# The rounding number of an FP4 quantiser: two VectorE passes, or one ScalarE pass and a fused maximum

## The chip, the core and the metric

The kernel runs on one core of a Trainium2 chip. A core has five engines that run side by side, each through its own queue of instructions: TensorE (PE in the profile; its weight loads are PEld), VectorE (DVE), ScalarE (ACT), GpSimd (POOL) and SyncE (SP, which here only issues DMAs). The metric is the device time of one execution in microseconds, the median of several runs.

## The reference, cut to what matters

The input x has 16 batches of 512 rows of 256 values. Each row is normalised to xn. From xn come two results: s, a layer of attention with 16 heads followed by a feed-forward layer with GELU, and g, a gated feed-forward layer in which every operand is first rounded to FP4 in blocks of 16 values. The output is x + s * g.

```python
xn = _layernorm(x, axis=-1)
s = _L0_attn_ref(xn, ...)                      # attention, then ffn_w1, gelu, ffn_w2
g = _silu(_L0_ffn_ref(xn, w_gate, w_up, w_down))
x = x + s * g

def fp4_quant_dequant(x):                      # blocks of 16
    scale = jnp.maximum(jnp.max(jnp.abs(xb), axis=-1, keepdims=True) / 6.0, 1e-12)
    xn = xb / scale
    idx = jnp.searchsorted(_MID, jnp.abs(xn))  # _MID 0.25, 0.75, 1.25, 1.75, 2.5, 3.5, 5
    q = _GRID[idx] * jnp.sign(xn) * scale      # _GRID 0, 0.5, 1, 1.5, 2, 3, 4, 6

gate, y = fp4_linear(x, w_gate), fp4_linear(x, w_up)
return fp4_linear(jax.nn.silu(gate) * y, w_down)   # 704 hidden columns
```

The part at issue is the rounding to the grid. After division by its block's scale a value lies between -6 and 6, and the grid's step there is 0.5 below 2, 1 from 2 to 4 and 2 above 4.

## The kernel before, in words

The work is cut into 64 steps. Step s handles batch b = s // 4 and g = s % 4; g counts both four heads of the attention and one of the four tiles of 128 rows of the gated layer. In the same step the previous batch ("old") goes through the later parts of its layer: its attention output and first normalisation at g = 0 and 1, the expansion by ffn_w1 with GELU (`expand`) at g = 1 and 2, and the contraction by ffn_w2 at g = 2 and 3.

One step goes like this. TensorE first multiplies the attention weights of the step before with the values (`context`, tile cp), and ScalarE copies that out (`kept`, tile ct). Then come five bursts: the scores of this step (`weights`: tile ws, of which there is one buffer; ScalarE takes its exponential into pr, and GpSimd multiplies pr by a table, `tabled`), and the scores of the next step (`maxima`: tile ms; VectorE takes its maxima, whose throw-away output is called junk). Between bursts the letters of a plan (`PLAN[g]`) put other pieces, such as the transposes ctp and ct of `output`, xqtp of `turned_x` and hqtp of `turned_hidden`. At the end of the step come the gated layer's two halves (`hidden`: tiles gp, up and gu; ScalarE's Silu writes sl, VectorE multiplies into wide), the first stage of their quantiser, the product with the down weights of the step before (`gate`: tile dp, ScalarE writes gated), for g = 1 and 2 of an old batch `expand`, then a dummy exponential (`expect`, tile ready) that has the table for Exp loaded in good time, and last the remaining stages of the quantiser.

The quantiser is `fp4_stages`, a generator in four stages. It takes the block maxima (amax) and their reciprocal (inv) on VectorE and multiplies by inv on GpSimd (L222); then it makes the rounding number m, adds it, subtracts it, and multiplies by the block's scale on GpSimd (L232). Adding and subtracting a large number rounds a value to that number's last place, so m has to follow the value's size: m is the value's power of two, but at least 1, times 6291456. VectorE makes it in two passes, a bitwise "and" that keeps the exponent (L226) and a maximum with a multiplication (L227). In `ROUNDING`, three of the four tiles of a batch have the addition and the subtraction on VectorE ("dd"); the fourth (g = 3) has the subtraction on GpSimd ("dg"). The tile m has one buffer for all quantisers.

The quantiser works on the hidden values (tile wide, 128 x 704) once in every step; on the inputs of the gated layer (tile xq, 128 x 512, two row tiles at once) in every second step, started at g = 1 and g = 2; and on the weights (tiles wide and raw_d) while the kernel starts up.

What sets the order: TensorE issues in the order in which the program is written throughout, and from step 0 on VectorE and ScalarE do too (`dve.fixed = act.fixed = True`). An instruction that waits on one of these engines therefore holds up all that follow it there. GpSimd, SyncE, and the start-up before step 0 are ordered by a scheduler at build time. Nearly all instructions of the three ordered engines pass through one helper, so the profile shows them with its line, L72, and they are told apart by their tiles.

Of the kernel before, what the change touches and what calls it, by code (L numbers as in the profile page):

```python
# [11 lines left out]

F32 = mybir.dt.float32
I32 = mybir.dt.int32
F32R = mybir.dt.float32r
BF16 = mybir.dt.bfloat16
AF = mybir.ActivationFunctionType
ALU = mybir.AluOpType
# [7 lines left out]
I_FF = 704  # L26
D_FF = 4 * D
ALPHA, MIX, STEP_A = 3.0, 0.15, 6.0
P = 128
# [12 lines left out]

ROUND = 12582912.0
TURN = 6.283185
LEVEL = 6291456.0
EXPONENT = 0x7F800000
UNDER = 1.0 + 2.0**-22


# [1 line left out]
def tile_block(ctx: ExitStack, tc: tile.TileContext, a: dict, pos: bass.AP, win: bass.AP, out: bass.AP):  # L51
    nc = tc.nc
# [21 lines left out]
    pe, dve, act = InOrder(nc.tensor, True), InOrder(nc.vector, False), InOrder(nc.scalar, False)  # L74
# [20 lines left out]
    sb = ctx.enter_context(tc.tile_pool(name="sb", bufs=1))  # L95
# [82 lines left out]
    NF = D_FF // P  # L178
# [14 lines left out]

    v_aug = [keep.tile([P, NT, H, VS], F32, name=f"va{i}", tag=f"va{i}") for i in range(2)]

    def fp4_stages(dst, src, n, width, engines=(dve, dve)):

        nb = width // 16
        widest = 2 * D if width <= 2 * D else I_FF

        def temporary(name, columns):
            return sb.tile([P, widest // columns], F32, name=f"{name}{widest}", tag=f"{name}{widest}")[
                :n, : width // columns
            ]

        amax, scale, inv = (temporary(x, 16) for x in ("amax", "scale", "inv"))

        def blocks(t):
            return t.rearrange("p (n k) -> p n k", k=16)

        def per_block(t):
            return t.unsqueeze(2).to_broadcast([n, nb, 16])

        dve.tensor_reduce(amax, blocks(src), AX.X, ALU.max, apply_absolute_value=True)
        dve.tensor_scalar(inv, amax, UNDER / 6.0, UNDER * 1e-12, ALU.mult, ALU.max)  # L220
        dve.reciprocal(inv, inv)
        nc.gpsimd.tensor_tensor(blocks(dst), blocks(src), per_block(inv), ALU.mult)  # L222
        nc.gpsimd.tensor_scalar(scale, amax, 1.0 / 6.0, 1e-12, ALU.mult, ALU.max)  # L223
        yield
        m = sb.tile([P, I_FF], F32, name="m", tag="m")[:n, :width]
        dve.tensor_scalar(m.bitcast(I32), dst.bitcast(I32), EXPONENT, None, ALU.bitwise_and)  # L226
        dve.tensor_scalar(m, m, 1.0, LEVEL, ALU.max, ALU.mult)  # L227
        yield
        engines[0].tensor_tensor(dst, dst, m, ALU.add)
        yield  # L230
        engines[1].tensor_tensor(dst, dst, m, ALU.subtract)
        nc.gpsimd.tensor_tensor(blocks(dst), blocks(dst), per_block(scale), ALU.mult)  # L232

    def fp4(dst, src, n, width):
        for _ in fp4_stages(dst, src, n, width):
            pass
# [9 lines left out]
    def bank(name):  # L246
        return ps.tile([P, 512], F32, name=name, tag="mm")
# [335 lines left out]
    def turned_h(b, h, half):  # L583
        hT = sb.tile([P, NC, 2 * P], F32, name=f"hT_{b}_{half}", tag="hT")
        tp = bank(f"htp_{b}_{half}")
        for c in range(NC):
            for t in range(2):
                turn(tp[:, (2 * c + t) * P : (2 * c + t + 1) * P], rows_of(h, 2 * half + t)[:, c * P : (c + 1) * P])
        act.copy(hT.rearrange("p c t -> p (c t)"), tp)
        return hT  # L590

    def expand(b, half, hT):

        acts = []
        for f in range(NF):
            fp = bank(f"f1_{b}_{half}_{f}")
            for c in range(NC):
                mm(fp[:, : 2 * P], w1[:, c, f * P : (f + 1) * P], hT[:, c, :], start=(c == 0), stop=(c == NC - 1))
            acts.append(sb.tile([P, 2 * P], F32, name=f"act_{b}_{half}_{f}", tag="act", bufs=NF + 2))
            act.activation(acts[f], fp[:, : 2 * P], AF.Gelu, bias=fb1[:, f : f + 1])  # L600
        return acts
# [33 lines left out]

    HI = I_FF // 2

    ROUNDING = [[dve if e == "d" else nc.gpsimd for e in by] for by in ("dd", "dd", "dd", "dg")]

    def quantised(b, t):  # L640

        xq = sb.tile([P, 2, D], F32, name=f"xq_{b}_{t}", tag="xq", bufs=2)
        src = xns[b][t // 2].rearrange("p t d -> p (t d)")
        return xq, fp4_stages(xq.rearrange("p t d -> p (t d)"), src, P, 2 * D)
# [10 lines left out]
    def hidden(b, t, xqT):  # L655

        hid = wide[t % 2]

        def halves():
            for s in range(2):  # L660
                cut = slice(s * HI, (s + 1) * HI)
                if s == 1:
                    both = ps_s.tile([P, 2, S], F32, name=f"gu_{b}_{t}", tag="ws")
                    gp, up = both[:, 0, :], both[:, 1, :]
                else:
                    gp, up = bank(f"gp_{b}_{t}"), bank(f"up_{b}_{t}")
                for wT, acc in ((wgT, gp), (wuT, up)):
                    for c in range(NC):
                        mm(
                            acc[:, :HI],  # L670
                            xqT[:, c * P : (c + 1) * P],
                            wT[:, c, cut],
                            start=(c == 0),
                            stop=(c == NC - 1),
                        )
                sl = sb.tile([P, HI], F32, name=f"sl_{b}_{t}_{s}", tag="sl", bufs=2)
                act.activation(sl, gp[:, :HI], AF.Silu)
                dve.tensor_tensor(hid[:, cut], up[:, :HI], sl, ALU.mult)
                yield

        return hid, halves(), fp4_stages(hid[:, :I_FF], hid[:, :I_FF], P, I_FF, ROUNDING[t])

    def turned_hidden(b, t, hq):
        hqT = sb.tile([P, NI, P], F32, name=f"hqT_{b}_{t}", tag="hqT")
# [15 lines left out]
    def expect(function):  # L700

        act.activation(ready, mhalf[:, 0:1], function)
# [291 lines left out]
    for k in range(H // 2 + 2):  # L994
# [14 lines left out]
        if 0 < k < H // 2 + 1:  # L1009
            tag, bufs = (("pr1", 1), ("gated", 2))[k % 2]  # L1010
# [26 lines left out]
    xq, stages = quantised(0, 0)  # L1037
# [66 lines left out]
    waiting, hq, cts, turned_hs, acts, coming, mv = None, None, [], {}, {}, None, None  # L1104
    xqTs, hqTs = {}, {}
    xqs = {0: xq}
    stages = iter(())
# [4 lines left out]
    for s in range(STEPS):  # L1112
        b, g = divmod(s, H // 4)
        old, has_old = b - 1, b > 0
# [61 lines left out]
        if pair and pair[0] < B:  # L1176
            xqs[(4 * pair[0] + pair[1]) // 2], more = quantised(*pair)
            next(more)
        hq, halves, stages = hidden(b, g, xqTs.pop((b, g)))
        before = (b, g)  # L1180
        ops = ahead
# [19 lines left out]
        if gating:  # L1201
            gate(*gating, hqTs.pop(gating))
        if has_old and g in (1, 2):
            acts[g - 1] = expand(old, g - 1, turned_hs[g - 1])
        if not has_old:
            for _ in stages:
                pass
# [3 lines left out]
        if s == NT - 1:  # L1211
            for w, name in ((w1, "ffn_w1"), (w2, "ffn_w2")):
                nc.sync.dma_start(out=w, in_=a[name].rearrange("(c p) n -> p c n", p=P))
        expect(AF.Exp)
        if s + 2 < STEPS:
            ahead = operands(*divmod(s + 2, H // 4))
# [4 lines left out]
    old = B - 1  # L1221
# [14 lines left out]
    hT = turned_h(old, h, 0)  # L1236
# [5 lines left out]
    for half in range(2):  # L1242
        acts[half] = expand(old, half, hT)
        if half == 0:
            hT = turned_h(old, h, 1)
        for i, _ in enumerate(contract(old, h, half, acts[half], mv, 1)):
            if i % 4 < 3:
                continue
            caught_up()
            t = 2 * half + i // 4  # L1250
            rs = sb.tile([P, 2], F32, name=f"rs_last_{t}", tag="rs2")
            inverse_deviation(rs[:, :1], mv[:, t : t + 1, 1])
            layernorm(rows_of(h, t), mv[:, t, 0:1], rs[:, :1], g2, b2)
            gt = gated[:, t, :]
            dve.tensor_tensor(gt, gt, rows_of(h, t), ALU.mult)
            dve.tensor_tensor(gt, gt, x_last[:, t, :], ALU.add)
            nc.sync.dma_start(out=out[old, t * P : (t + 1) * P, :], in_=gt)
# [43 lines left out]
```

## Time and profile before

| | |
|---|---|
| runs | 1875.64, 1875.63 and 1872.88 us, median 1875.63 us |
| span of the profiled execution, first to last instruction | 1872.6 us |
| TensorE busy, share of the span | 1774.8 us, 95% |
| VectorE busy | 1423.1 us, 76% |
| GpSimd busy | 1310.3 us, 70% |
| ScalarE busy | 1069.1 us, 57% |
| ScalarE table loads | 168, 215.5 us |
| rounding number on VectorE, 704 columns ("and"; maximum and product) | 65 x 854 ns; 66 x 809 ns |
| addition or subtraction, 704 columns, VectorE | 114 x 907 ns |
| subtraction on GpSimd (L231) | 16 x 1686 ns |

The page of the profile gives the profiled execution's span and not its total time; the span lies 0.28 us below the fastest of the three runs and 3.03 us below their median, so what lies around the span is at most about 3 us. A mean over the whole span mixes the start-up (until about 300 us), the repeating stretch of about 106 us for each batch, and the ending (the last 63 us). The lines of waits say which engine sat idle and which engine's instruction ended it; the idle time of an engine costs something only if the end of the kernel waits for it.

### The profile page before, as it was taken

Reading aid. Unit: us, or ns where it says so; the run is one execution under the profiler, and the core shown is the slowest. Engines: PE = TensorE matmul, PEld = TensorE weight load, DVE = VectorE, ACT = ScalarE, POOL = GpSimd, SP = SyncE. Lnnn points to the kernel's source line nnn. Section 1 sums busy time; section 2 is a strip of 40 time slices with the busy share of each in tenths; the row PEclk is TensorE's granted clock in tenths of the full one; section 3 lists DMA queues with packets and bytes.
Section 4 is the critical chain, followed back from the end, with each engine's and each line's share of the span. In section 5 each row is a group of like instructions: output and inputs, shape, how many; then the busy total and the mean of one; then the engine's idle time right before and its main releaser. Section 6 shows DMA issues by size and latency. Waiting matters only on the chain.

```text
span 1872.6 us, 31762 instructions
## 1 busy us (share of the span) xinstructions
PE 1774.8 (95%) x10411; PEld 1240.5 (66%) x10411; DVE 1423.1 (76%) x3887; ACT 1069.1 (57%) x1853; POOL 1310.3 (70%) x1128
## 2 busy tenths in 40 slices
PE   5679799999999999999999999999999999999998
PEld 2235467676776767676776767677676767677676
DVE  5878587787878777787878777787878778787754
ACT  5654455655665555556565565556555565565553
POOL 5467477767776776777676776777677776777671
PEclk8869799999999999999999999999999999999999
DMA  6344242432323242422334242332333242232200
GB/s 203 95 148 134 81 129 68 138 87 88 109 89 120 68 126 80 137 84 76 112 95 127 60 135 81 117 101 76 112 94 109 73 138 86 77 108 79 72 21 12
DMA packets 127114, 184.68 MB, mean 99 GB/s; under 512 B 15315, under 2 KB 57749, under 8 KB 126949
## 3 DMA queue, kind: packets, MB, share of 16 engines
q1 hardware_dynamic: 122496, 181.25, 32.2%
q8 instruction: 83, 1.36, 0.3%
q10 hardware_dynamic: 4004, 0.98, 0.3%
q14 instruction: 83, 0.67, 0.1%
q0 software_dynamic: 448, 0.42, 0.1%
HBM read 136.45 MB, written 45.09 MB: 97 GB/s over the span
## 4 chain that ended last, share of the span: by engine, by line
PE 81%; DVE 8%; POOL 1%; issue 1%; ACT 1%; DMA 0%; DVEq 0%; POOLq 0%; ACTq 0%
PE f L72 25%; PE dp L72 8%; PE gu L72 8%; PE cp L72 7%; PE ws L72 5%; DVE junk L72 4%; PE op L72 4%; PE gp L72 4%; PE up L72 4%; PE ms L72 4%; PE vp L72 3%; PE hqtp L72 2%; DVE cx L72 1%; PE qk_wk L72 1%; PE qk_wq L72 1%
## 5 line engine op out<-in xcount | busy, mean ns | idle before, releaser
L500 POOL TENSOR_TENSOR pr<-pr,table 128x1024 f32<-128x1024 f32 (+2 forms) x448 | 768.0, 1748 | 75.2 <-ACT pr L72 73.0
L72 DVE CUSTOM_DVE_ANT_0 junk<-ms,mask 128x512 bf16<-128x512 f32 (+3 forms) x1024 | 501.9, 490 | 231.9 <-PE ms L72 155.0
L72 ACT ACTIVATE pr<-ws 128x1024 f32<-128x1024 f32 (+1 forms) x350 | 327.0, 955 | 134.4 <-PE ws L72 129.1
L72 ACT ACT_TABLE_LOAD x168 | 215.5, 1283 | 64.3 <-PE gp L72 48.8
L72 PE MATMUL f<-w,act 128*128 128x256 f32 x1024 | 249.0, 387 | 0.0
L72 PE MATMUL f<-hT,w 128*128 128x256 f32 x1024 | 226.3, 380 | 0.0
L72 PEld LDWEIGHTS f<-hT,w 128*128 128x128 f32 x1024 | 194.8, 190 | 26.3 <-ACT hT L72 0.2
L72 PEld LDWEIGHTS f<-w,act 128*128 128x128 f32 x1024 | 187.0, 190 | 31.3
L232 POOL TENSOR_TENSOR wide<-wide,scale 128x704 f32<-128x704 f32 (+1 forms) x71 | 96.6, 1361 | 136.5 <-DVE wide L72 132.9
L72 PE MATMUL ws<-qT,kT 38*128 38x512 f32 (+3 forms) x1024 | 157.5, 371 | 21.4 <-ACT pr L72 16.5
L72 PE MATMUL dp<-wdT,hqT 128*128 128x256 f32 x768 | 176.2, 379 | 0.0
L72 PEld LDWEIGHTS dp<-wdT,hqT 128*128 128x128 f32 x768 | 146.1, 190 | 31.1 <-issue 6.7
L72 ACT ACTIVATE act<-f,fb 128x256 f32<-128x256 f32 x256 | 118.2, 474 | 75.3 <-PE f L72 72.5
L72 PE MATMUL ms<-kT,qT 36*128 36x512 f32 (+3 forms) x1024 | 145.1, 330 | 9.5 <-DMA kT<-k_d 6.3
L72 PE MATMUL cp<-pr,va 128*17 128x512 f32 (+3 forms) x2048 | 151.5, 434 | 0.0
L72 PEld LDWEIGHTS ws<-qT,kT 38*128 38x128 f32 x1024 | 81.6, 188 | 90.8 <-issue 51.7
L72 PEld LDWEIGHTS cp<-pr,va 128*17 128x17 f32 x2048 | 54.3, 97 | 99.4 <-issue 79.5
L223 POOL TENSOR_SCALAR scale<-amax 128x32 f32<-128x32 f32 (+1 forms) x104 | 37.0, 356 | 116.6 <-DVE amax L72 113.5
L72 DVE TENSOR_TENSOR wide<-wide,m 128x704 f32<-128x704 f32 (+2 forms) x126 | 112.4, 892 | 4.1
L222 POOL TENSOR_TENSOR wide<-wide,inv 128x704 f32<-128x704 f32 (+1 forms) x71 | 99.1, 1396 | 21.5 <-DVE inv L72 21.1
L72 PEld LDWEIGHTS ms<-kT,qT 36*128 36x128 f32 x1024 | 96.2, 189 | 18.4 <-issue 12.8
L72 DVE TENSOR_SCALAR m<-m 128x512 f32<-128x512 f32 (+1 forms) x104 | 102.6, 986 | 3.4
(217 smaller groups left out, 3009.5 us busy)
## 6 DMA issues: line engine op xcount, KB each, us to landing
table<-rv SPq DMA_DIRECT2D x64, 1024.0 KB
kT<-k_d SPq DMA_DIRECT2D x256, 76.0 KB
qT<-q_d SPq DMA_DIRECT2D x256, 72.0 KB
x<-in_L_attn_x_dram SPq DMA_DIRECT2D x21, 512.0 KB
q_d<-q_hi SPq DMA_DIRECT2D x32, 256.0 KB
q_d<-q_lo SPq DMA_DIRECT2D x32, 256.0 KB
k_d<-k_hi SPq DMA_DIRECT2D x32, 256.0 KB
k_d<-k_lo SPq DMA_DIRECT2D x32, 256.0 KB
```

The source lines that it names most:

```text
L72: return lambda *args, **kw: self.follow(op(*args, **kw))
L222: nc.gpsimd.tensor_tensor(blocks(dst), blocks(src), per_block(inv), ALU.mult)
L223: nc.gpsimd.tensor_scalar(scale, amax, 1.0 / 6.0, 1e-12, ALU.mult, ALU.max)
L232: nc.gpsimd.tensor_tensor(blocks(dst), blocks(dst), per_block(scale), ALU.mult)
L500: nc.gpsimd.tensor_tensor(part, part, table[:, mine, j * P :], ALU.mult)
```

## The change

ScalarE makes the rounding number: one activation, the absolute value with the scale 4194304, written in bfloat16. The floor that the maximum gave moves into VectorE's addition and subtraction, which become fused instructions of the form (m max 5242880) op value. The subtraction now yields the negative of the rounded value, so GpSimd makes the block's scale negative. `ROUNDING` is gone; both fused instructions are on VectorE in every step. ScalarE's instruction is also given a place of its own in the step: with g = 1 and 2 of an old batch it stands between the fourth and the fifth GELU of `expand`; with g = 0 and 3 it stands after `gate` and ahead of the dummy exponential; in the first batch it runs with the rest of the quantiser, behind `gate`. The quantiser of xq runs its stages where it did, so there the new instruction stands on ScalarE behind the second Silu of `hidden`.

```diff
-LEVEL = 6291456.0
-EXPONENT = 0x7F800000
+LEVEL = 4194304.0
...
-        nc.gpsimd.tensor_scalar(scale, amax, 1.0 / 6.0, 1e-12, ALU.mult, ALU.max)
+        nc.gpsimd.tensor_scalar(scale, amax, -1.0 / 6.0, -1e-12, ALU.mult, ALU.min)
         yield
-        m = sb.tile([P, I_FF], F32, name="m", tag="m")[:n, :width]
-        dve.tensor_scalar(m.bitcast(I32), dst.bitcast(I32), EXPONENT, None, ALU.bitwise_and)
-        dve.tensor_scalar(m, m, 1.0, LEVEL, ALU.max, ALU.mult)
+        m = sb.tile([P, I_FF], BF16, name="m", tag="m")[:n, :width]
+        act.activation(m, dst, AF.Abs, scale=LEVEL)
         yield
-        engines[0].tensor_tensor(dst, dst, m, ALU.add)
+        dve.scalar_tensor_tensor(dst, m, 1.25 * LEVEL, dst, ALU.max, ALU.add)
         yield
-        engines[1].tensor_tensor(dst, dst, m, ALU.subtract)
+        dve.scalar_tensor_tensor(dst, m, 1.25 * LEVEL, dst, ALU.max, ALU.subtract)
         nc.gpsimd.tensor_tensor(blocks(dst), blocks(dst), per_block(scale), ALU.mult)
...
-    def expand(b, half, hT):
+    def expand(b, half, hT, between=iter(())):
         acts = []
         for f in range(NF):
+            if f == NF // 2:
+                next(between, None)
...
-    ROUNDING = [[dve if e == "d" else nc.gpsimd for e in by] for by in ("dd", "dd", "dd", "dg")]
...
-        return hid, halves(), fp4_stages(hid[:, :I_FF], hid[:, :I_FF], P, I_FF, ROUNDING[t])
+        return hid, halves(), fp4_stages(hid[:, :I_FF], hid[:, :I_FF], P, I_FF)
...
-            acts[g - 1] = expand(old, g - 1, turned_hs[g - 1])
+            acts[g - 1] = expand(old, g - 1, turned_hs[g - 1], stages)
...
+        if not has_old or g % 3 == 0:
+            next(stages, None)
         expect(AF.Exp)
```

More of the change, by code (lines that the diff above doesn't have):

```diff
@@ L13 @@
 F32 = mybir.dt.float32
-I32 = mybir.dt.int32
 F32R = mybir.dt.float32r
@@ L194, in tile_block, with fp4_stages @@
     v_aug = [keep.tile([P, NT, H, VS], F32, name=f"va{i}", tag=f"va{i}") for i in range(2)]
-    def fp4_stages(dst, src, n, width, engines=(dve, dve)):
+    def fp4_stages(dst, src, n, width):
         nb = width // 16
```

## The prediction, made before the changed kernel was run

> **What bounds the kernel now.** I read the page's busy line and the windows first, then TensorE's waits, then time lines of single engines.
>
> ```profile
> PE 1774.8 (95%) x10411; PEld 1240.5 (66%) x10411; DVE 1423.1 (76%) x3887; ACT 1069.1 (57%) x1853; POOL 1310.3 (70%) x1128
> 100.00:150.00 50.00, 39.95 (x199) 22.70 (x196) 39.29 (x107) 29.68 (x72) 37.56 (x37) 0.75 0.45 137
> 830.00:936.00 106.00, 104.17 (x635) 74.77 (x634) 83.50 (x231) 62.45 (x104) 78.03 (x63) 1.00 0.34 100
> ```
>
> The windows' columns are the stretch, then PE, PEld, DVE, ACT and POOL busy, clock and DMA. In a repeating batch TensorE is busy for 104.17 of 106.0 us, so whatever VectorE, ScalarE and GpSimd gain can return at most 1.8 us of a batch. During the start-up TensorE idles a fifth of the time. TensorE's waits from 300 to 1784 us say what the 1.8 us are:
>
> ```profile
> PE ws L72 <- ACT pr L72: 11.1, 15, 0.8
> PE ct L72 <- DVE mx L72: 10.2, 26, 0.5
> PE ct L72 <- DVE cx L72: 2.6, 13, 0.2
> ```
>
> In each batch there is one wait of 0.8 us for ScalarE's exponential and about three of 0.2 to 0.5 us for VectorE; none names the quantiser. The change can therefore gain little in a batch, and the question is what it makes later.
>
> **The price of the pieces.** The rows by form give, for 704 columns:
>
> ```profile
> L72 DVE TENSOR_SCALAR m<-wide 128x704 int32<-128x704 int32 x65 | 55.5, 854 | 33.4 <-POOL wide L222 29.0
> L72 DVE TENSOR_SCALAR m<-m 128x704 f32<-128x704 f32 x66 | 53.4, 809 | 2.3
> L72 DVE TENSOR_TENSOR wide<-wide,m 128x704 f32<-128x704 f32 x114 | 103.3, 907 | 3.9
> ```
>
> Removed from VectorE: 854 + 809 = 1.66 us a step, and 367 + 1321 = 1.69 us for each xq. In a batch that is 4 x 1.66 + 2 x 1.69 = 10.0 us. From GpSimd 1.69 us goes (L231, g = 3), for which VectorE gets one more pass of 0.91.
>
> Added on ScalarE: an activation from SBUF takes 629 ns for 512 columns (pos_sb) and 1051 ns for 1024 (sines), 0.82 ns a column, so 0.79 us for 704 and 0.63 for 512; 4 x 0.79 + 2 x 0.63 = 4.4 us a batch. The two fused instructions don't occur with these types. At 512 columns the fused form on rest takes 678 ns and the addition on xq 708, so I take 0.91 us. The lower end is 0.87 (907 x 678 / 708). A fused pass on xn stretched from 0.48 to 1.10 us beside GpSimd's work, but at the narrowest place below GpSimd idles, waiting for these very passes; the upper end is 1.1. Their places in VectorE's queue stay.
>
> No run here shows Abs. Either it needs no table load, or a load before it and one after, 1.28 us each; I take none, because Copy and Identity stand among Exp and Silu in this trace without one. The Trainium skill, "ScalarE: Activation LUTs", section "Table sets: the hidden batching unit", says that abs is in every set; no row here shows it, and without that sentence the third rival's +131 us would stand beside the sum as it is. The rules for kernel authors on that page speak against this change: maxima and products belong on VectorE, which it has as the faster engine. In this trace the two undisturbed VectorE passes take 0.53 + 0.53 us where I estimate one ScalarE pass at 0.79.
>
> **From g = 3 to the next batch's g = 0,** the narrowest place. ScalarE, then VectorE:
>
> ```profile
> 870.03 0.38 ACT L72 ACTIVATE gated<-dp 128x256 f32<-128x256 f32 x1 [1.23 <-PE dp L72]
> 870.43 1.28 ACT L72 ACT_TABLE_LOAD   x1
> 871.73 0.20 ACT L72 ACTIVATE ready<-mhalf 128x1 f32<-128x1 f32 x1
> 872.34 0.59 ACT L72 COPY ct<-cp 128x512 f32<-128x512 f32 x1 [0.41 <-PE cp L72]
> ...
> 868.98 1.03 DVE L72 TENSOR_SCALAR m<-wide 128x704 int32<-128x704 int32 x1 [1.50 <-POOL wide L222]
> 870.61 0.89 DVE L72 TENSOR_TENSOR wide<-wide,m 128x704 f32<-128x704 f32 x1
> 872.98 0.69 DVE L72 CUSTOM_DVE_ANT_0 junk<-ms,mask 128x512 bf16<-128x512 f32 x1 [1.48 <-PE ms L72]
> ```
>
> Its input is there (GpSimd ends at 868.95), so Abs runs from 870.41 to 871.20. Behind it queue the table load, ready, the copy ct and the exponentials. The cover is the copy's wait of 0.41 us; 0.79 - 0.41 = 0.38 us comes through. It delays the transposes of ct, and the burst of ws that waits for the second exponential:
>
> ```profile
> 875.79 0.50 PE L72 MATMUL ws<-qT,kT 38*128 38x384 f32 x4 [0.78 <-ACT pr L72]
> 878.32 0.44 PE L72 MATMUL ct<-ident,cx 128*128 128x128 f32 x2 [0.49 <-DVE mx L72]
> ```
>
> The first wait becomes 1.16 us. But the second, 2.5 us on, is for VectorE, whose work from 872.98 on has no gap; if VectorE isn't later, TensorE waits 0.11 there instead of 0.49, and the 0.38 is taken up. VectorE's addition now waits for Abs: 871.20, 872.11, end of the subtraction 873.02 + 0.05 for signals, against the 872.98 at which junk starts. So about 0.1 us remains; with the fused passes at 1.1 it would be 0.4. From the first batch's end on there are 15 such places: **+1.5 us**, with ends 0 and 15 x 0.38 = 5.7.
>
> **The other three places** I cost at nothing. From g = 0 to 1 ScalarE's exponential waits 0.81 us for ws (at 896.78); 0.79 fits into that with 0.02 to spare. VectorE ends its subtraction at 897.1 instead of 895.8, and its next work starts at 897.60. GpSimd's scale ends at 898.5, 0.6 us into its first table product, and GpSimd has gaps of 0.34 and 0.66 us before TensorE needs the last product at 922. At g = 1 and 2 Abs stands among GELUs with gaps of 0.39 us behind four of them, 1.56 in all; the last GELU isn't moved. For xq, ScalarE waits 2.1 us for dp at that point. The one buffer of m is no wait: VectorE's xq passes end near 918.5, and Abs comes at 919.6. With a cover gone, each place costs up to 0.79 a batch.
>
> **The ending.** In the last step Abs waits for GpSimd, which is where it bites:
>
> ```profile
> 1821.59 0.38 ACT L72 ACTIVATE gated<-dp 128x256 f32<-128x256 f32 x1 [2.13 <-PE dp L72]
> 1821.99 1.28 ACT L72 ACT_TABLE_LOAD   x1
> 1823.89 0.59 ACT L72 COPY ct<-cp 128x512 f32<-128x512 f32 x1 [0.41 <-PE cp L72]
> 1825.96 0.25 DVE L72 RECIPROCAL rinv<-ctp 128x16 f32<-128x16 f32 x1
> ```
>
> GpSimd's product ends at 1823.49. Abs then runs to 1824.3, the load and ready (1.28 + 0.20) to 1825.8, ct to 1826.4, four transposes to 1826.7: rinv comes 0.7 us later, and the chain of waits to the end runs through it. **+0.7 us**, ends 0 and 1.6.
>
> **The start-up** is a balance of small shifts. TensorE waits 9.49 us at 59.10 for a weight tile whose way holds m passes of 0.43, 0.43 and partly 1.16 us on VectorE: -0.7. From 76.5 to 93.7 VectorE is full and four m passes (0.29 + 0.29 + 0.43 + 0.73 = 1.74 us) leave it, but TensorE's ms is ready at most 0.95 earlier, and Abs delays ScalarE's copy of the kernels, which has 0.32 us to spare: -0.3. At the end of step 1 Abs must wait for GpSimd (158.8), ends at 159.6 and delays pooled_row by 0.6 us; through a DMA this reaches the exponential for which TensorE waits at 167.71, but at 168.92 TensorE then no longer waits 0.48 us for VectorE: +0.1. Elsewhere 0, as at the end of step 0, where TensorE waits 4.91 us for a DMA. Sum **-0.9 us**. A scheduler orders most of this part, so the ends are wide: -5.5 (the second rival) and +4 (six weight passes of 0.63 us on a ScalarE that has no gap).
>
> **Sum**: 1.5 + 0.7 - 0.9 = +1.3 us on the span of 1872.6, 1873.9. What lies around the span is left as it is (at most 3.0 us by the median), so on the median 1875.63 + 1.3 = **1876.9 us**.
>
> **Rivals.** *ScalarE becomes the wait* (slower): the 0.38 us isn't taken up at ct, since VectorE is late too. Then 15 x 0.38 + 0.7 - 0.9 = +5.5, 1881.1 us. For: ScalarE has no gap from 872.34 to 880.8; the spare 0.02 us at the next place is nothing. Against: the 0.49 us wait stands in every batch. It decides as soon as junk starts over 0.3 us later than TensorE's ms allows. *The start-up gains* (faster): VectorE is the fullest engine beside TensorE there, and at the end of step 1 (157 to 164 us) its chain loses 3.65 us of m passes (0.36 + 1.50 + 0.53 + 1.26) for one Abs of 0.79. With -1.0, -1.7 and -2.8 at the three places named and nothing in the batches: -5.5 + 0.7 = -4.8, 1870.8 us. It decides if the scheduler puts Abs ahead of ScalarE's statistics. Against: TensorE's waits there name DMAs, ScalarE and ms more than m. *Abs needs its own tables*: at g = 0 and 3 one more load each, less the 0.81 and 0.41 us of cover, 1.26 + 1.66 us; at g = 1 and 2 two loads and 0.79 against 1.56 of gaps, 1.8 each; for xq two loads and 0.63 against 2.1, 1.1 each: 8.7 x 15 = +131, about 2007 us.
>
> **Chances.** Two runs of this kernel differ by up to 0.15%; about 0.2%, 3.75 us, is what can be told from no change. Forecast 0.50, with its own range 1872.5 to 1880; ScalarE as the wait 0.28; start-up gain 0.18; tables 0.02; the rest 0.02. Same takes 0.37 of the forecast, 0.03 of the first rival and 0.02 of the second, 0.42; slower takes 0.25 of the first rival, 0.08 of the forecast, the tables' 0.02 and 0.01 of the rest, 0.36; faster takes 0.16 of the second rival, 0.05 of the forecast and 0.01 of the rest, 0.22. The range runs from 1869.5 (the second rival with 1.3 us for the spread of the runs) to 1886 (the upper ends, 5.7 + 4, with the ending's 0.7).
>
> **What would show it.** Right: in a batch VectorE's busy time falls from 83.5 to about 74.4 us, ScalarE's rises from 62.4 to about 66.9, TensorE's stays at 104.2; ct starts 0.3 to 0.4 us later behind ready at g = 0, ws <- pr grows to about 1.2 us and ct <- mx shrinks to 0.1. Wrong: more than 168 table loads; a batch that grows by over 0.3 us; a new wait of junk for the subtraction; or a start-up whose first full batch begins over 4 us off.

## The result: slower by 0.2 to 0.35%, and the profile after

Measured beside the kernel before, the changed kernel took 1881.7 us against 1875.5 (medians of six runs each, ratio 1.0035, 95% interval 1.0024 to 1.0046). Measured once more in a later set it came to 1878.9 us, ratio 1.0021 (1.0009 to 1.0032). It is a small loss, with a wide spread: the changed kernel's own runs lie between 1875.0 and 1885.3 us, those of the kernel before in that later set between 1871.8 and 1876.7. The forecast was 1876.9 us. Two disturbed executions, one of the changed kernel in the later set and one of an experiment, are left out of the ranges and ratios.

The profiled execution after has a span of 1881.4 us, 8.8 more than the one before. It belongs to one of the slower runs (1883.1 us, 1.7 us more than its span), so this pair differs by more than the medians do. Its page and its windows, read as before (stretch, PE, PEld, DVE, ACT, POOL, clock, DMA), show the work itself moved as foreseen:

```profile
PE 1778.4 (95%) x10411; PEld 1242.5 (66%) x10411; DVE 1300.0 (69%) x3695; ACT 1129.2 (60%) x1957; POOL 1275.9 (68%) x1112
```

```profile
100.00:150.00 50.00, 38.86 (x179) 20.98 (x177) 34.26 (x91) 28.96 (x67) 35.14 (x33) 0.70 0.37 108
830.00:936.00 106.00, 104.23 (x635) 74.68 (x634) 75.81 (x220) 66.00 (x110) 75.93 (x63) 1.00 0.33 100
```

In a repeating batch VectorE is busy for 75.81 instead of 83.50 us and ScalarE for 66.00 instead of 62.45. TensorE stays at 104.23 of 106. TensorE's waits from 300 to 1784 us are the same three lines, hardly longer:

```profile
PE ws L70 <- ACT pr L70: 13.7, 17, 2.3
PE ct L70 <- DVE mx L70: 8.3, 26, 0.3
PE ct L70 <- DVE cx L70: 2.6, 13, 0.2
```

The rows by form price the new instructions, and the last line counts the table loads, 168 as before. Abs needs none:

```profile
L70 ACT ACTIVATE m<-wide 128x704 bf16<-128x704 f32 x65 | 50.9, 784 | 15.3 <-POOL wide L220 9.2 <-DVE xq L70 5.8 <-ACT act L70 0.3
L70 DVE SCALAR_TENSOR_TENSOR wide<-m,wide 128x704 f32<-128x704 bf16 x130 | 119.8, 922 | 144.0 <-ACT m L70 141.8
L70 DVE SCALAR_TENSOR_TENSOR xq<-m,xq 128x512 f32<-128x512 bf16 x64 | 75.2, 1176 | 1.3 <-ACT m L70 0.2
L70 ACT ACT_TABLE_LOAD x168 | 215.5, 1283 | 65.2 <-PE gp L70 49.5
```

So where do 8.8 us go? A batch can be timed from one qk_wq, the first projection of a batch, to the next. A quiet batch takes 106.09 us in both traces, and the thirteen periods from 248 us (256 after) on add up to 1384.1 us before and 1382.7 after: nothing is lost there (three of the periods before and two after are some 1.6 us longer, each by one drop of TensorE's clock). Up to mp of step 0 (94.3 us before, 94.2 after) nothing is lost either. From there to the same mp in the middle of the second batch (the transpose of the next step's maxima at g = 1) it is 177.9 us before and 184.3 after, so 6.4 us go in the first batch and the first steps of the second. Up to the second batch's first qk_wq it is even 7.8 us (248.16 and 255.97); 1.5 of them the kernel before gives back at 262 us, by one of its own drops of the clock. Of the 7.8 us, 3.0 come up to the mp in step 3 (224.73 and 227.76 us) and 4.8 between that mp and the next one. The last step, from its gated to the end of the span, takes 51.75 instead of 51.01 us, 0.74 more. The 1.65 us that are left between these and the ending are one drop of TensorE's clock near 1655 us (0.68 from 1653 to 1658 us, where the kernel before has 1.00 at the same stage); such drops come up again below.

### The profile page after: what moved, and what is told of

The parts are those of the page before. It is cut to its first block, busy times and chain, and to the rows that moved or that the text cites. A ratio compares the mean times of both kernels' runs of the same rounds, so it can differ in the third digit from the quotient of the medians.

```text
span 1881.4 us, 31449 instructions
## 1 busy us (share of the span) xinstructions
PE 1778.4 (95%) x10411; PEld 1242.5 (66%) x10411; DVE 1300.0 (69%) x3695; ACT 1129.2 (60%) x1957; POOL 1275.9 (68%) x1112
## 4 chain that ended last, share of the span: by engine, by line
PE 78%; DVE 6%; ACT 5%; POOL 1%; issue 1%; DMA 1%; POOLq 0%; DVEq 0%; ACTq 0%
PE f L70 25%; PE dp L70 8%; PE gu L70 8%; PE ws L70 5%; PE cp L70 5%; PE op L70 4%; PE gp L70 4%; PE up L70 4%; PE ms L70 3%; PE vp L70 3%; DVE junk L70 2%; PE hqtp L70 2%; ACT pr L70 2%; PE qk_wk L70 1%; PE qk_wq L70 1%; ACT L70 1%
## 5 line engine op out<-in xcount | busy, mean ns | idle before, releaser
L70 DVE SCALAR_TENSOR_TENSOR wide<-m,wide 128x704 f32<-128x704 bf16 (+1 forms) x142 | 129.3, 911 | 148.7 <-ACT m L70 146.3
L220 POOL TENSOR_TENSOR wide<-wide,inv 128x704 f32<-128x704 f32 (+1 forms) x71 | 107.3, 1511 | 25.5 <-DVE inv L70 21.2
L70 ACT ACTIVATE sl<-gu 128x352 f32<-128x352 f32 x64 | 29.6, 463 | 119.6 <-PE gu L70 119.6
```

The costliest lines, as they stand in the source:

```text
L70: return lambda *args, **kw: self.follow(op(*args, **kw))
```

## Experiments

The theory: an instruction that stands in ScalarE's order ahead of the exponential's table load, and that waits there for GpSimd, delays ct and the exponentials of the next step. In a repeating batch its input is long there; in the first batch and in the last step it is not. The rivals: the steady batches pay for it, or the part before step 0 does. In the repeating batch the place that the prediction called the narrowest looks like this (ScalarE first, then VectorE; a batch of the changed kernel):

```profile
876.62 0.38 ACT L70 ACTIVATE gated<-dp 128x256 f32<-128x256 f32 x1 [1.23 <-PE dp L70]
876.90 0.78 ACT L70 ACTIVATE m<-wide 128x704 bf16<-128x704 f32 x1
877.70 1.28 ACT L70 ACT_TABLE_LOAD   x1
879.10 0.57 ACT L70 COPY ct<-cp 128x512 f32<-128x512 f32 x1
...
877.71 1.82 DVE L70 SCALAR_TENSOR_TENSOR wide<-m,wide 128x704 f32<-128x704 bf16 x2 [3.65 <-ACT m L70]
879.57 0.69 DVE L70 CUSTOM_DVE_ANT_0 junk<-ms,mask 128x512 bf16<-128x512 f32 x1
```

Abs waits for nobody there. At the end of the first batch's last step it does, and TensorE waits for ct, which it did not before:

```profile
233.03 0.38 ACT L70 ACTIVATE gated<-dp 128x256 f32<-128x256 f32 x1 [1.15 <-PE dp L70]
234.56 0.79 ACT L70 ACTIVATE m<-wide 128x704 bf16<-128x704 f32 x1 [1.16 <-POOL wide L220]
235.37 1.28 ACT L70 ACT_TABLE_LOAD   x1
236.78 0.57 ACT L70 COPY ct<-cp 128x512 f32<-128x512 f32 x1
...
237.40 0.77 PE L70 MATMUL ctp<-ident,ct 128*128 128x128 f32 x5 [0.98 <-ACT ct L70]
```

What follows it costs more than the 0.98 us. The windows of 240 to 250 us, first before, then after (the clock is the third number from the end):

```profile
240.00:245.00 5.00, 5.00 (x30) 3.77 (x29) 4.23 (x20) 2.79 (x5) 5.00 (x4) 1.00 0.20 55
245.00:250.00 5.00, 5.00 (x17) 2.79 (x16) 3.53 (x9) 2.10 (x4) 4.84 (x5) 1.00 0.17 58
```

```profile
240.00:245.00 5.00, 4.79 (x24) 4.31 (x24) 2.94 (x12) 3.25 (x7) 5.00 (x3) 0.50 0.39 122
245.00:250.00 5.00, 5.00 (x24) 3.81 (x23) 2.77 (x11) 2.11 (x4) 3.34 (x4) 0.51 0.02 3
```

TensorE is busy nearly all the time and works at half its clock. (The kernel before reaches the same instructions some 3 us earlier; its clock is at 1.00 from 235 to 240 us too.)

**Which part of the kernel?** Four kernels put the old and the new form together by parts. Each calls the quantiser with a form for the weights, for the first batch and for the rest (the edit is shortened here); the order of TensorE's instructions is the same in all.

```diff
-    def fp4_stages(dst, src, n, width):
+    def fp4_stages(dst, src, n, width, form="abs", engines=None):
...
+        if form == "two passes":          # m by "and", maximum and product on VectorE, as before
+            dve.tensor_scalar(m.bitcast(I32), dst.bitcast(I32), 0x7F800000, None, ALU.bitwise_and)
+            dve.tensor_scalar(m, m, 1.0, 6291456.0, ALU.max, ALU.mult)
...
+FORM_W = "abs"                            # gate and up weights
+def form_h(b, t):                         # the first batch old, the rest new
+    return "two passes" if b == 0 else "abs"
```

> The changed kernel, but the quantisers of the first batch's four hidden tiles, of the three xq made in or ahead of it and of the down weights have VectorE's two passes again; gate and up weights and everything from the second batch on stay changed. Theory (the lost time comes from ScalarE's in-order Abs in the first batch, about 5 us of the 6.2 between the medians 1875.5 and 1881.7; the rest is a step 0 that starts 1.4 us late and about 1 us in the ending): about 1877.5 us. Rival A (the steady batches or the ending cost it): 1881 us. Rival B (it is the start-up ahead of step 0, by its late start): 1880 to 1881 us.

> The kernel before up to the end of the first batch; the changed quantiser only from the second batch on, ending included. Theory (steady batches cost nothing, the last step about 1 us): 1876.5 us, a batch period of 106.1 us as in both kernels, and the first qk_wq within 1 us of the kernel before (248.2 us). Rival A (steady batches or ending cost the 6.2 us): 1881 us.

> The reverse: the changed quantiser in the start-up and the first batch, VectorE's two passes from the second batch on. Theory (start-up and first batch hold the loss): about 1880.7 us, and the second batch's start about 7 us later than the kernel before. Rival A (steady batches or ending): 1875.5 to 1876.5 us.

> The changed quantiser only for the gate and up weights, before step 0; everything else as before. The scheduler orders this part, and in this kernel it issues SyncE's DMAs as in the changed kernel: the 1 MB table of step 1 ahead of the small rows (qT<-mhi, qT<-mlo) that step 0 waits for. Theory (Abs in the first batch is the larger part): step 0 starts 1.4 us late and 1 to 1.5 us of it lasts, 1876.5 to 1877 us. Rival B (the late start, by whatever it sets off in the first batch, is the whole loss): 1880 to 1881 us. Rival C (the fused passes gain time here, as the weights' wait predicted): 1875 us or less.

| changed quantiser in | median, us | ratio to the kernel before, 95% interval |
|---|---|---|
| second batch to the end only | 1874.63 | 1.0000 (0.9991 to 1.0008) |
| gate and up weights only | 1876.81 | 1.0011 (1.0002 to 1.0020) |
| weights, and second batch to the end | 1876.41 | 1.0010 (1.0001 to 1.0019) |
| weights and first batch | 1877.86 | 1.0014 (1.0006 to 1.0023) |

The first line rules out the steady batches and the ending as the larger part of the loss; the ending's 0.7 us are in it and lie within its interval. The weights alone cost something; the first batch, by these medians, little more than 1 us, and the parts together 2.4 us, less than was first measured for the whole. The theory's 5 us for the first batch were therefore not shown, and the whole kernel was run again.

> The changed kernel once more, unaltered, beside the three others of this set. The parts measured so far do not add up to it: gate and up weights +1.7 us, second batch onwards -0.4, weights and first batch +2.8, so all three together would be about +2.4, 1877.5 us, where the first measurement had 1881.7 (six runs from 1875.3 to 1885.3, the longer the lower their mean clock, .975 to .966). Theory (the parts add, and six runs of a widely spread kernel put the median too high): 1877 to 1879 us. Rival (first batch and second batch together cost more than each, by a clock step that only the whole sets off): 1881 to 1882 us.

1878.9 us, ratio 1.0021. It lies at the upper end of the theory's range: part of the first 1881.7 was the spread of a kernel whose runs differ by 10 us. The spread goes with the clock: each run has its mean granted clock on record, 0.974 or 0.975 for this kernel's runs of about 1875 us and 0.966 for the one of 1885.3. A straight line through time and clock of the runs behind the ratios, with one slope for all kernels, gives an estimate of what is left at an equal clock: both measurements of the changed kernel then agree, some 3 us above the kernel before. The parts' sum, 2.4 us, is near the 3.7 of this set and within its interval of 1.7 to 6.0.

**Only Abs added.** The kernel before, with nothing removed, and seven Abs on ScalarE whose output nobody reads.

```diff
+            if form == "both":            # first batch and last step, at the changed kernel's places
+                act.activation(sb.tile([P, I_FF], BF16, name="dead", tag="sl", bufs=2)[:n, :width], dst, AF.Abs, scale=LEVEL)
             dve.tensor_scalar(m.bitcast(I32), dst.bitcast(I32), 0x7F800000, None, ALU.bitwise_and)
```

> The kernel before with nothing taken from VectorE or GpSimd: seven Abs are only added on ScalarE, into a tile that nobody reads, at the places where the changed kernel has them in the first batch (four hidden tiles, two xq) and in the last step. Theory (an Abs that waits in ScalarE's queue for GpSimd holds up the exponential's table load, ct and the exponentials behind it): the first batch's end (the second batch's gu at g = 0) 3 to 5 us later than in the kernel before, the last step 1 us longer, 1877 to 1880 us. Rival (the first batch's loss comes from the new VectorE passes or from another order of work, not from ScalarE's queue): within 0.5 us of the kernel before, 1875 to 1875.5 us.

1880.0 us, ratio 1.0027 (1.0016 to 1.0039). From mp of step 0 to mp in the second batch it takes 184.1 us, as in the changed kernel (184.3; before 177.9), and the last step takes 51.72 us. The same wait and the same half clock stand at the same place:

```profile
233.56 0.79 ACT L70 ACTIVATE dead<-wide 128x704 bf16<-128x704 f32 x1 [1.16 <-POOL wide L220]
236.40 0.77 PE L70 MATMUL ctp<-ident,ct 128*128 128x128 f32 x5 [1.00 <-ACT ct L70]
```

```profile
240.00:245.00 5.00, 5.00 (x28) 4.45 (x28) 1.73 (x8) 3.51 (x7) 5.00 (x3) 0.50 0.30 104
```

Seven instructions in ScalarE's order make a loss of this size by themselves; VectorE's new passes are not needed for it.

**Abs behind the dummy exponential.** If the wait in ScalarE's order is the cause, work that needs no input can fill it.

```diff
+        if not has_old or s == STEPS - 1:
+            expect(AF.Exp)
         if not has_old:
             for _ in stages:
                 pass
...
-        expect(AF.Exp)
+        if not (not has_old or s == STEPS - 1):
+            expect(AF.Exp)
```

> The changed kernel, but in the first batch's steps and in the last step the dummy exponential (with its table load of 1.28 us) stands ahead of the quantiser's Abs on ScalarE instead of behind it, so that it fills the time in which Abs waits for GpSimd. Theory: ct comes up to 1.2 us earlier at the ends of steps 0, 1, 2 and 3 and in the last step; TensorE then does not stop for 1 us at 237 us, its granted clock stays at 1.00 in 240 to 250 us instead of 0.50; 3 to 4 us less than the changed kernel of this set and about 1 us of it in the ending. Rival (the clock step has another cause, the order on ScalarE does not matter): as the changed kernel of this set.

1873.75 us, ratio 0.9994 (0.9985 to 1.0002): 5 us less than the changed kernel of its set. ScalarE now has its table loaded when wide comes, and ct follows Abs at once:

```profile
231.16 0.38 ACT L70 ACTIVATE gated<-dp 128x256 f32<-128x256 f32 x1 [1.15 <-PE dp L70]
231.55 1.28 ACT L70 ACT_TABLE_LOAD   x1
232.95 0.77 ACT L70 ACTIVATE m<-wide 128x704 bf16<-128x704 f32 x1
233.63 0.57 ACT L70 COPY ct<-cp 128x512 f32<-128x512 f32 x1
```

```profile
240.00:245.00 5.00, 5.00 (x33) 3.81 (x32) 3.49 (x17) 3.42 (x7) 5.00 (x4) 0.76 0.02 3
245.00:250.00 5.00, 5.00 (x20) 3.42 (x21) 4.19 (x17) 2.71 (x4) 4.92 (x5) 1.00 0.30 79
```

The clock still drops, but for a shorter time, and the last step takes 51.15 us instead of 51.75. The stretch from mp to mp is 179.4 us. The expectation of a clock at 1.00 throughout was too good, that of the time too modest.

**The DMAs ahead of step 0.** The kernel with changed weights alone showed a second cause. SyncE's queue is ordered by the scheduler at build time, and with other instructions for the weights it issued two tables of 1 MB, of steps 0 and 1, one behind the other at 90 us, ahead of the rows of 4 KB that step 0's first scores need. Before, only the first stood ahead of them. TensorE's first ws, in the kernel before, in the changed one, and in one with the old order of the DMAs:

```profile
97.47 0.79 PE L72 MATMUL ws<-qT,kT 38*128 38x512 f32 x2 [2.82 <-DMA qT<-mlo]
```

```profile
98.91 0.80 PE L70 MATMUL ws<-qT,kT 38*128 38x512 f32 x2 [4.27 <-DMA qT<-mlo]
```

```profile
94.92 0.80 PE L70 MATMUL ws<-qT,kT 38*128 38x512 f32 x2 [2.83 <-DMA qT<-mlo]
```

```diff
         load = nc.sync.dma_start(out=table, in_=...)
+        if (b, g) == (0, 1):
+            tc.add_manual_dep(load.ins, small[0, 0].ins.name, in_order, reason="behind the rows")
```

> The changed kernel with the order of SyncE's DMAs ahead of step 0 as in the kernel before: the 1 MB table of step 1 is issued behind the small rows (qT<-mhi, qT<-mlo) that step 0's first scores wait for; everything else stays as in the changed kernel. Theory (that order, which the scheduler chose otherwise because the weights' instructions changed, makes step 0 start late): TensorE's wait ahead of the first ws falls from 4.3 to about 2.8 us and the kernel is 1 to 1.5 us faster than the changed kernel of this set. Rival (the wait is taken up by later ones, such as the table of step 1 that now comes later): within 0.5 us of it.

1875.6 us, ratio 1.0010 (1.0001 to 1.0018), against 1.0021 for the changed kernel of its set; the intervals of the two overlap. The wait falls by 1.44 us, as expected, but in the profile little of it is gained. In both kernels ScalarE then stands until rows of x have landed, and TensorE waits for the exponential behind that. The changed kernel first, then the one with the old order:

```profile
110.10 0.50 PE L70 MATMUL ws<-qT,kT 38*128 38x384 f32 x4 [0.17 <-ACT pr L70]
```

```profile
106.38 0.50 PE L70 MATMUL ws<-qT,kT 38*128 38x384 f32 x4 [2.93 <-ACT pr L70]
```

A stretch at half clock follows (0.52 from 107.5 to 111 us), and from mp of step 0 to the next mp 22.66 us pass instead of 22.85. So 0.2 of the 1.44 us are left there, which speaks for the rival; that this order costs time at all is not shown by itself. At an equal clock, by the estimate above, the two kernels are less than half a microsecond apart.

**Both repairs, and each part of the gain taken back.**

> The changed kernel with both repairs: the dummy exponential ahead of Abs in the first batch's steps and the last step, and the table of step 1 issued behind the rows of step 0. Theory (the two are apart in time and add): the 1873.75 us of the first repair less the 1.44 us by which the rows' wait falls (4.27 to 2.83), about 1872.3 us, 0.15% below the kernel before. Rival (the start of step 0 decides nothing, the later waits take it up): as with the first repair alone, 1873.5 to 1874 us.

> As the kernel with both repairs, but the first batch's quantisers have VectorE's two passes again (gate and up weights and the second batch onwards keep Abs). Theory (with the repair, Abs in the first batch costs next to nothing, but gains nothing either): within 1.5 us of the kernel with both repairs. Rival (Abs still holds up the first batch): 2 us or more faster than it, 1870 us.

> As the kernel with both repairs, but gate and up weights have VectorE's two passes; everything up to step 0 is then as in the kernel before. Theory (the weights' part gains a little by itself: over six profiles the first mp comes at 93.8 us on average with Abs and at 94.3 with two passes): 0.5 us slower than the kernel with both repairs, and a narrower spread. Rival (the weights' part costs, as the 1876.8 us of the kernel with only the weights changed seemed to say, even without the order of the DMAs): 1 us or more faster.

With both repairs the kernel takes 1871.5 us, ratio 0.9986 (0.9977 to 0.9995): faster than both kernels. Its interval overlaps that of the first repair alone (0.9985 to 1.0002), so what the second one adds is not shown. With two passes in the first batch it takes 1875.8 (1.0006, 0.9997 to 1.0015), with two passes for the weights 1874.6 (0.9996, 0.9987 to 1.0005). So, repaired, the first batch gains by Abs (the two intervals just miss each other) where the expectation was that it would neither cost nor gain; for the weights the intervals overlap and no gain is shown. Where the first batch gains the 4 us between the medians is only in part seen. From the mp in step 1 to the one in step 2 the three kernels with Abs behind the dummy exponential take 30.1 us, the five with two passes in the first batch 31.9 to 33.7. The rest stays open: the two profiles differ from mp to mp by 1.6 us only (176.8 and 178.4), and in that stretch the one with two passes has a drop of the clock (0.66 from 260 to 265 us) that the other has not.

All these traces together show most plainly what the order on ScalarE costs at the end of the first batch. The stretch from the mp in step 3 to the next one, in the kernel before, in the changed one, and in the one with the first repair:

```profile
224.73:245.69 20.96, 19.69 (x133) 13.26 (x132) 15.09 (x50) 14.48 (x25) 13.66 (x9) 1.00 0.54 167
```

```profile
227.76:253.49 25.73, 23.80 (x133) 16.71 (x132) 15.49 (x50) 16.57 (x27) 15.26 (x11) 0.80 0.45 136
```

```profile
225.89:248.31 22.42, 21.56 (x132) 14.39 (x131) 14.93 (x49) 15.41 (x26) 14.33 (x10) 0.92 0.49 153
```

It takes 21.0 us in all five kernels whose first batch has two passes and no Abs, 24.1 to 25.8 in the five with Abs ahead of the dummy exponential, and 22.4 in the three with Abs behind it. TensorE's wait of 1.0 us for ct stands in every one of the second five and in none of the others.

**What the cover is worth.** The steady batches lose nothing; how near are they to losing?

```diff
-            act.activation(m, dst, AF.Abs, scale=LEVEL)
+            for _ in range(2 if form == "abs twice" else 1):     # g = 0 and 3, from the second batch on
+                act.activation(m, dst, AF.Abs, scale=LEVEL)
```

> The changed kernel, but from the second batch on Abs runs twice (the same instruction repeated) at g = 0 and g = 3, except in the last step: one more ScalarE pass of 0.79 us at each of the two places. It prices the cover. Theory (from g = 3 to 0 at most 0.3 us of the wait for VectorE's mx is left as cover, and from g = 0 to 1 0.02 us of the wait for ws): 0.5 to 0.8 us a place, 15 batches, so +8 to +12 us from the first place and up to +12 from the second, 10 to 24 us slower than the changed kernel (1879 to 1882). Rival (TensorE's order has more slack than its waits show, ScalarE's work is hidden there): within 2 us of the changed kernel.

1910.1 us, ratio 1.0187 (1.0173 to 1.0201), four runs: about 30 us slower than the changed kernel, more than the theory's upper end of 24 (the 1879 to 1882 us in the expectation are the changed kernel's own times). A quiet batch takes 107.25 us, 1.16 more, which is within the theory; but nine of the thirteen periods are over 108 us, where two were over 107.5 in the changed kernel. TensorE's waits from 300 to 1784 us, and a batch of each kind:

```profile
PE ws L70 <- ACT pr L70: 26.5, 55, 3.3
PE ctp L70 <- ACT ct L70: 7.7, 14, 0.6
```

```profile
579.03:686.28 107.25, 104.34 (x636) 74.49 (x635) 75.56 (x221) 67.56 (x112) 76.22 (x62) 1.00 0.33 99
686.28:795.08 108.80, 105.90 (x635) 75.76 (x634) 75.89 (x221) 67.62 (x112) 76.36 (x62) 0.98 0.32 98
```

The 1.6 us between the two is again the clock. Six of the nine drops stand about 14 us into the batch, as in the changed kernel, and three some 97 us into it, where that kernel has none.

## Why the prediction was right or wrong, by its steps

**The mix of the batch**: right. ScalarE's 66.00 us against some 66.9; no table load, as the page "ScalarE: Activation LUTs" of the Trainium skill ("Table sets: the hidden batching unit") says of abs, and the 168 loads agree. VectorE came to 75.81 us instead of 74.4: the fused pass of xq was put at 0.91 us and takes 1.18. That term was mis-sized, and the time does not notice.

**From g = 3 to g = 0**: right in mechanism, with a remainder that measured nothing. The copy ct was to come 0.38 us later and comes about 0.15 later, measured from its batch's start (90.76 against 90.61), because Abs starts 0.10 us before gated's 0.38 us are over, and ct 0.09 us before ready's 0.20. The first wait was to grow from 0.78 to 1.16 us and stays; the second gives the 0.15 back:

```profile
882.53 0.50 PE L70 MATMUL ws<-qT,kT 38*128 38x384 f32 x4 [0.78 <-ACT pr L70]
884.91 0.44 PE L70 MATMUL ct<-ident,cx 128*128 128x128 f32 x2 [0.33 <-DVE mx L70]
```

VectorE's junk starts as early in its batch as before (91.23 us against 91.25), as the sum of the two fused passes had it. The remainder of 0.1 us a batch, +1.5 in all, is 0 in the periods.

**The other three places**: right as far as the periods show it, which do not grow. A second pass at g = 0 and one at g = 3 together cost 1.16 of their 1.57 us a batch, so these two covers were real and nearly used up; those at g = 1 and 2 and of xq were not tried.

**The ending**: right. +0.7 us was forecast and 51.75 - 51.01 = 0.74 us measured. The wait that makes it, ScalarE's for GpSimd and TensorE's for ct (0.23 us in the kernel before):

```profile
1831.67 0.79 ACT L70 ACTIVATE m<-wide 128x704 bf16<-128x704 f32 x1 [1.63 <-POOL wide L220]
1833.88 0.57 ACT L70 COPY ct<-cp 128x512 f32<-128x512 f32 x1
1834.50 1.64 PE L70 MATMUL ctp<-ident,ct 128*128 128x128 f32 x13 [2.13 <-ACT ct L70]
```

**The start-up**: this is the step that failed: -0.9 us, with an upper end of +4, against 6.4 us from mp to mp in the profiled pair and, by the medians of the whole (+3.7 and +6.2) less the ending's 0.74, some 3 to 5.5. The prediction's own sign of being wrong, a first full batch that begins over 4 us off, came true by the 7.8 us. Three things were missing. First, "Elsewhere 0": the ends of the first batch's steps were not read like the last step, although Abs waits there for GpSimd or VectorE in the same way (1.16 us at 234 us). Added alone, those Abs and the last step's cost 4.8 us between the medians. Second, only TensorE's and ScalarE's orders were followed; that the scheduler would put a 1 MB table ahead of the rows on SyncE's queue was not thought of; it made one wait 1.44 us longer, of which only 0.2 us came back at the next mp with the old order. Third, no term had the clock in it: a wait of 1 us was priced at 1 us, and the stretch that holds it and the half clock behind it, from the mp in step 3 to the next one, took 4.8 us more (25.73 against 20.96), though TensorE sat idle for only 0.6 us more of it (1.9 against 1.3). The other 3.0 of the 7.8 us are, on balance, those of step 1 (from the mp in step 0 to the one in step 1 38.8 against 35.7 us) and stay open; the kernel that is as before until the second batch takes 37.2 there, so half of it can be the spread. The one place that was worked out behind it, TensorE's wait of 1.55 us at 167.71, grew to 2.1 us as foreseen. The part before step 0 that was worked out, -0.7 and -0.3, is neither shown nor refuted: mp of step 0 comes at 93.8 us on average over nine profiles with Abs for the weights, at 94.5 over the four with two passes, but single ones lie between 91.7 and 97.3. And that the measured times stay within the stated range of 1869.5 to 1886 us is partly luck: the +4 us that the start-up was allowed were put there for six weight passes, not for what came.

**The rivals**: "ScalarE becomes the wait" had the sign and nearly the time, 1881.1 us, but not the place: it put the loss into the fifteen steady places, and with those alone changed there is none. "The start-up gains" has the sign of what is measured with both repairs, 3.3 us between the medians against its 4.8; that it comes by the chain which that rival names is not shown. Of the two medians one lies in the forecast's own range, to 1880 us, and the other above it.

## What to carry to other kernels

Ask of every instruction that is put into an engine's fixed order not what it costs in the repeating batch but when its input comes in the first one and the last one, and put work without an input, such as a table load, ahead of it. When instructions of a part that a scheduler orders are changed, compare the order of the DMA queues too: a large transfer ahead of a small one is a wait that no instruction list of the engines shows (1.44 us here, though the next wait took most of it up). And a wait of the engine that is 95% busy is not worth its length alone where the clock can fall behind it.

## What the runs showed of the hardware

TensorE's clock falls to half after waits that are far shorter than the drop. Two batches of the changed kernel, 13 us into each, TensorE's order and its waits the same up to there (0.20 us for cx and 0.30 for mx):

```profile
375.08:380.08 5.00, 4.70 (x24) 3.73 (x23) 2.71 (x12) 2.23 (x6) 4.78 (x4) 0.66 0.34 114
801.34:806.34 5.00, 4.71 (x44) 3.78 (x44) 3.97 (x17) 3.46 (x8) 5.00 (x4) 1.00 0.30 107
```

In one the clock is at 0.50 for some 3.4 us and the batch is 1.6 us longer, in the other not. The kernel before has such batches as well, three of thirteen. In the kernel with Abs twice, with waits of 0.43 and 0.37 us in the 4 us ahead of that place, it happened there in six of thirteen. The page "TensorE: Matmul & The Clock Gate" of the Trainium skill ("HAM oscillation — how this bites in real kernels") gives as its rule that TensorE should have no idle gap of over about 3.4 us. Here the waits ahead of the drop were of 0.2 to 0.4 us each, and of 0.98 us at 237 us.

What differs between the two batches can be read from the record of the clock in the traces. In each of the thirteen that are used here, all stretches at 0.50 begin on one grid with steps of 3.413 us and last a whole number of steps, but for the last, which ends with the trace. In the changed kernel's fourteen batches from 256 us on the drops come at 376.2, 1014.5 and 1652.8 us, each 187 steps behind the one before. In these three batches a point of the grid lies 13.9 to 14.1 us behind the batch's start; in the other eleven the first one behind 12.3 us lies at 14.2 to 15.7. In the thirteen traces together, every batch of this stretch with a point between 13.3 and 14.1 us is hit. So which batch is hit depends on where the grid happens to lie. How long TensorE idles in one step of the grid doesn't decide it alone: 0.56 us in the step ahead of the drop at 376.2 us, while in the kernel before a step with 1.25 us (97 us into its batch) has none behind it. First the two steps around that drop, then the step without one:

```profile
372.79:376.20 3.41, 2.85 (x19) 1.81 (x19) 3.09 (x9) 2.93 (x5) 3.41 (x2) 0.99 0.91 256
376.20:379.61 3.41, 3.41 (x14) 2.70 (x14) 1.73 (x9) 0.84 (x3) 3.41 (x3) 0.50 0.18 64
```

```profile
555.10:558.51 3.41, 2.16 (x20) 1.78 (x20) 2.91 (x12) 3.01 (x6) 3.41 (x2) 1.00 0.50 154
```

That the short waits cause the drops is argued from their number and their place; no run shows it by itself.

The clock differs as much in the part before step 0, where the changed kernel and the one with the old order of the DMAs have the same instructions in the same order until 87 us:

```profile
25.00:40.00 15.00, 13.43 (x27) 5.95 (x28) 12.77 (x23) 11.32 (x34) 5.40 (x9) 0.60 0.64 197
```

```profile
25.00:40.00 15.00, 11.26 (x30) 4.39 (x31) 12.99 (x24) 13.89 (x40) 6.37 (x11) 0.89 0.65 201
```

Their mp of step 0 lies 2.5 us apart (94.25 and 91.71 us). Single profiles of whole executions therefore cannot settle differences of this size; medians over six to eleven runs settle the larger ones.
